# An LSTM beside an FFN on one core: four gates in one PSUM bank, cell operands in the other, weight sums on GpSimd

## The chip, the cores and the metric

The kernel runs on one core of a Trainium2 chip. A core has a matrix engine (TensorE, "PE" in the profile, with its weight loads as "PEld"), VectorE ("DVE"), ScalarE ("ACT"), GpSimd ("POOL") and a queue engine for transfers (SyncE, "SP"). They work side by side and wait for each other through semaphores. SBUF is the on-chip working memory; PSUM is a smaller one of eight banks of 512 fp32 columns on 128 partitions, into which TensorE writes its sums. The metric is the device time of one execution in microseconds; the kernel before takes 307.32 us (median of 3 runs, 306.71 to 307.52).

## What is computed

An LSTM of 64 steps over 32 sequences with 256 features, then a three-layer FFN whose weights are +1 or -1 on every output of the LSTM, and a residual. Cut to what matters:

```python
def step(carry, xw_t):                    # xw_t = x_t @ Wx + b
    prev_h, prev_c = carry
    a = xw_t + prev_h @ Wh                # 32 x 1024: gates i, f, o, g of 256 each
    i, f, o = sigmoid(a[:, :H]), sigmoid(a[:, H:2*H]), sigmoid(a[:, 2*H:3*H])
    g = tanh(a[:, 3*H:])
    next_c = f * prev_c + i * g
    next_h = o * tanh(next_c)
    return (next_h, next_c), next_h
...
h = concatenate([y, -y])                  # y: the LSTM's outputs
h = relu(s0 * (h @ W0)) * 2               # W: +1 / -1 from booleans
h = relu(s1 * (h @ W1)) * 2               # 1024 x 1024
return x + s2 * (h @ W2)
```

## The kernel before

**Layout.** The 256 features of a state are four quarters `q` of 64 columns. A quarter lies on 32 partitions (one for each sequence), so a cell tile is 128 partitions x 64 columns. The gate products of a step take the transposed state `hT` as 32-column weights and stream columns of `wh` past them; quarter `q` writes partitions 32q to 32q+31, so four such products run in TensorE beside each other. The gates stand in the order g, i, f, o (`GATES`, L60), each of 64 columns.

**Two gate banks.** `gate_banks` (L301) are two whole PSUM banks. The first holds g, i and f (192 columns used), the second o (64 columns). `gates_from_x` (L317) lets ScalarE copy the input's share of the step, `xg`, into both banks ahead of time (L319, L320), and `gates_from_h` (L304) adds `h @ Wh` onto it (L308): for each bank, each half `k` of the contraction and each quarter `q` one product, 16 a step. TensorE does an fp32 product in two passes, and the trace has a record for each. `cell_step` (L322) follows: the sigmoids of i and f (`sig`, L325), the tanh of g (`cand`, L326), the sigmoid of o (L327) on ScalarE; `kept` = f * c (L329), `new` = i * g (L331), their sum `c` (L333) on VectorE; `th` = tanh(c) on ScalarE (L335); `h` = o * th (L337) and its transpose into `hist` (L342) on VectorE. All tiles of the cell are in SBUF.

**What fills the time beside the recurrence.** The loop over t (L767) writes the engines' order by hand: each step issues its gate products and its cell, then as many pieces of other work as bring `done` up to a `goal` proportional to t. Up to step 20 (`X_STEPS` is 21) that is the products of x with Wx (`x_products`, L275; products of 128x256 at L249, evicted by `evict_x`, L261). From step 21 on it is the FFN (L777): four blocks of 16 time steps, with the layers at L425, L679 and L666. An FFN activation is kept as two fp32r parts, high and low, and each weight meets both. `split_h` (L347) makes the two parts of four steps of history: the high part on ScalarE (L361), the low part by a subtraction on VectorE (L362). The last two blocks (`last_blocks`, L442) do the second layer with fewer products: they use sums and differences of quarters of `w1`, which `make_sum` (L401) forms on VectorE, 16 instructions of 128x512 (L418).

**Small jobs.** `load` (L240) counts VectorE's extra work in a step. Splits and other small jobs go out where it is under 2; sums of w1 go out last in a step, from step 28 (`SUM_STEP`) on, while it is under 2 (L799 to L801). GpSimd does only the scalars and a few small loads at the start.

After step 63 nothing of the recurrence is left, and the rest of `last_blocks` runs to the end. There the two gate banks serve as product banks (`four_banks`, L446).

Of the kernel before, what the change touches and what calls it, by code (L numbers as in the profile page):

```python
# [34 lines left out]
F32 = mybir.dt.float32  # L35
F32R = mybir.dt.float32r
U8 = mybir.dt.uint8
AF = mybir.ActivationFunctionType
ALU = mybir.AluOpType
# [4 lines left out]
def lstm_ffn(ctx: ExitStack, tc: tile.TileContext, x, cond, wx_d, wh_d, b_d, k0_d, k1_d, k2_d, s0_d, s1_d, s2_d, out):  # L44
    nc = tc.nc
    P = 128
    N, T, D = x.shape
# [3 lines left out]
    HQ = H // NQ  # L51
# [6 lines left out]
    SH = 4  # L58
# [4 lines left out]
    X_STEPS = 21  # L63
# [5 lines left out]
    SUM_STEP = 28  # L69
# [7 lines left out]
    cell = ctx.enter_context(tc.tile_pool(name="cell", bufs=2))  # L77
# [6 lines left out]
    def act(shape, dtype, name):  # L84
        return apool.tile(shape, dtype, tag="act", name=name)
# [77 lines left out]
    for i in range(2):  # L163
        t = act([P, 2, F0], U8, f"k0_{i}")
# [75 lines left out]
    load = [0]  # L240
# [58 lines left out]
    hist, hparts = {}, {}  # L299

    gate_banks = [ps_g.tile([P, TB], F32, tag=f"gates{n}", name=f"gates{n}") for n in (3, 1)]  # L301
    gates = [g[:, : n * HQ].rearrange("p (g j) -> p g j", j=HQ) for g, n in zip(gate_banks, (3, 1))]

    def gates_from_h(t, hT):  # L304
        for g, slots in zip(gates, (slice(0, 3), slice(3, 4))):
            for k in range(2):
                for q in range(NQ):
                    nc.tensor.matmul(  # L308
                        g[q * N : (q + 1) * N],
                        hT[:, k, :],  # L310
                        wh_q[:, k, q, slots],
                        start=False,
                        stop=(k == 1),
                        skip_group_check=True,
                    )

    def gates_from_x(t):  # L317
        x_t = xg[t // 2 * 2][:, t % 2].rearrange("p (g j) -> p g j", g=4)
        nc.scalar.copy(gates[0], x_t[:, :3])  # L319
        nc.scalar.copy(gates[1], x_t[:, 3:])  # L320

    def cell_step(t, c):  # L322
        sig = cell.tile([P, 3, HQ], F32, tag="sig", name=f"sig{t}")
        cand = cell.tile([P, HQ], F32, tag="cand", name=f"cand{t}")
        nc.scalar.activation(sig[:, 0:2, :], gates[0][:, 1:3], AF.Sigmoid)  # L325
        nc.scalar.activation(cand, gates[0][:, 0], AF.Tanh)  # L326
        nc.scalar.activation(sig[:, 2, :], gates[1][:, 0], AF.Sigmoid)  # L327
        kept = cell.tile([P, HQ], F32, tag="kept", name=f"kept{t}")
        nc.vector.tensor_mul(kept, sig[:, 1, :], c)  # L329
        new = cell.tile([P, HQ], F32, tag="new", name=f"new{t}")  # L330
        nc.vector.tensor_mul(new, sig[:, 0, :], cand)  # L331
        c = cell.tile([P, HQ], F32, tag="c", name=f"c{t}")
        nc.vector.tensor_add(c, kept, new)  # L333
        th = cell.tile([P, HQ], F32, tag="th", name=f"th{t}")
        nc.scalar.activation(th, c, AF.Tanh)  # L335
        h = cell.tile([P, HQ], F32, tag="h", name=f"h{t}")
        nc.vector.tensor_mul(h, sig[:, 2, :], th)  # L337
        i, s = divmod(t, SH)
        if s == 0:
            hist[i] = hpool.tile([P, 2, SH * N], F32, tag="hist", name=f"hist{i}")  # L340
        hT = hist[i][:, :, ts(s, N)]
        nc.vector.transpose(hT, h.rearrange("p (j b) -> p b j", b=2))  # L342
        if t + 1 < T:
            gates_from_x(t + 1)
        return c, hT

    def split_h(i):  # L347

        b, s = divmod(i, SB // SH)
        if s == 0:  # L350
            hparts[b] = (
                hpool.tile([P, 2, TB], F32R, tag="hhi", name=f"hhi{b}"),
                hpool.tile([P, 2, TB], F32R, tag="hlo", name=f"hlo{b}"),
            )
        hi, lo = (p[:, :, ts(s, SH * N)] for p in hparts[b])
        full = hist.pop(i)
        if b == NB - 1:

            hi, lo = (a.rearrange("p k (n t) -> p k t n", n=N) for a in (hi, lo))
            full = full.rearrange("p k (t n) -> p k t n", n=N)  # L360
        nc.scalar.copy(hi, full)  # L361
        nc.vector.tensor_tensor(lo, full, hi, ALU.subtract)  # L362


    def evict(p, name):
# [35 lines left out]
    def make_sum(s, k):  # L401

        a11, a21 = w1[:, k, :F2], w1[:, k, F2:]
        a12, a22 = w1[:, K2 + k, :F2], w1[:, K2 + k, F2:]
        if s == 4:
            if k == 0:

                sums[s] = wpool.tile([P, K2, F2], F32R, tag="wx", name="s4")
            t = sums[s][:, k]
        else:  # L410
            t = act([P, F2], F32R, f"s{s}_{k}")
        in0, in1, op = {
            1: (a21, a22, ALU.add),
            2: (sums.get((1, k)), a11, ALU.subtract),
            3: (a11, a21, ALU.subtract),
            4: (a12, sums.get((2, k)), ALU.subtract),
        }[s]
        nc.vector.tensor_tensor(t, in0, in1, op)  # L418
        sums[s, k] = t

    f, parts = {}, {"b11": {}, "b21": {}}
# [294 lines left out]
    c = cell.tile([P, HQ], F32, tag="c", name="c_first")  # L716
# [28 lines left out]
    for _ in x_products(SB // 2, AHEAD):  # L745
        pass
    gates_from_x(0)


    def ffn():  # L750
        for b in range(NB - 2):
            yield from ffn_block(b)
        yield from last_blocks(NB - 2)
# [6 lines left out]
    sum_parts = deque(lambda s=s, k=k: make_sum(s, k) for k in range(K2) for s in range(1, 5))  # L760
# [6 lines left out]
    for t in range(T):  # L767
        load[0] = 0
        gates_from_h(t, hT)
        c, hT = cell_step(t, c)  # L770
        if t % SH == SH - 1:
            splits.append(t // SH)
        if outputs:
            load[0] += 1
            if next(outputs[0], "end") == "end":
                outputs.popleft()
        if t == X_STEPS:  # L777
            work, done = ffn(), 0
        goal = (t + 1) * total_x // X_STEPS if t < X_STEPS else (t + 1 - X_STEPS) * total_ffn // (T - X_STEPS)
        while done < goal:  # L780
            left_over[0] = goal - done
            done += next(work)
        if t == X_STEPS - 1:
            next(work, None)

        if turns and load[0] < 2:
            next_x(turns.popleft())
        if splits and (load[0] < 2 or t == T - 1 or t == SH * splits[0] + 2 * SH - 1):
            split_h(splits.popleft())
        else:  # L790
            if t >= FIRST_CHORE and chores:
                part = chores.popleft()()
                if part is not None:
                    w0_parts.append(part)
            elif t >= W2_STEP and chores2:
                chores2.popleft()()
            if w0_parts and (load[0] < 2 or t == X_STEPS - 1):
                w0_parts.popleft()()
            while sum_parts and t >= SUM_STEP and load[0] < 2:  # L799
                load[0] += 1  # L800
                sum_parts.popleft()()  # L801
    assert not sum_parts
    for _ in work:
        if outputs and next(outputs[0], "end") == "end":
# [29 lines left out]
```

## Time and profile before

| | |
|---|---|
| median of 3 runs | 307.32 us (306.71 to 307.52) |
| the profiled execution | 307.09 us, span 305.3 us from the first to the last instruction |
| granted TensorE clock | 1.000 |
| stretch to 16.7 us | start, loads, first products of x |
| 16.7 to 80.1 us | steps 0 to 20, beside the products of x |
| 80.1 to 231.4 us | steps 21 to 62, beside the FFN (step 63 begins at 231.4) |
| 231.4 to 300.6 us | the last blocks without the recurrence |
| VectorE busy in 80.1 to 231.4 | 88.1 of 151.3 us |
| ScalarE busy in 80.1 to 231.4 | 80.7 of 151.3 us |
| GpSimd busy after 12 us | nothing until the closing semaphores |

How to read the views: the page gives each engine's busy time, share of the span and number of instructions, and then the chain of work that ended last, by engine and line. The chain in order of time has start, length and what ran. A row of the groups has line, engine, operation, output<-inputs, shape and count, then busy us, mean ns of one, and the idle time before it. A row of the timeline has start, length, engine, line, operation, output<-input, shapes, and in brackets how long the engine had been idle before and what it waited for. Matmuls are pipelined: a row's length holds its latency too, and the distance between starts is what it costs.

### The profile page before, as it was taken

The numbers are of one execution on the slowest core, as the hardware profiler recorded it, in microseconds if no ns is written. First come the engines' busy times: TensorE is split into PE (matmuls) and PEld (weight loads), VectorE is DVE, ScalarE is ACT, GpSimd is POOL, SyncE is SP. The second block draws the span as 40 slices with busy tenths as digits, with TensorE's granted clock in tenths as the row PEclk, the third lists the DMA queues.
The fourth block names the chain that finished last, engine by engine and source line by source line (L and its number), as shares of the span: only waits on it lengthen the run. The fifth ranks groups of instructions, "written<-read, shape, count | busy, mean of one in ns | idle before, by whom it ended". The sixth has DMA issues, their size and how long they took to land.

```text
span 305.3 us, 9553 instructions
## 1 busy us (share of the span) xinstructions
PE 299.3 (98%) x4010; PEld 233.8 (77%) x4010; DVE 187.8 (62%) x527; ACT 154.9 (51%) x526; POOL 6.6 (2%) x24
## 2 busy tenths in 40 slices
PE   8999999999999999999999999999999999999993
PEld 4988887787777777777777777777777888888893
DVE  2476767676774565666575746444456689796341
ACT  0224657784565654444453544655676688644100
POOL 5300000000000000000000000000000000000000
PEclk9999999999999999999999999999999999999999
DMA  6865001133000000000001000000001330000012
GB/s 182 210 181 114 20 10 48 32 84 84 4 0 2 2 2 1 2 2 1 2 2 38 19 18 2 0 2 3 3 0 37 91 83 0 0 0 2 0 51 88
DMA packets 27450, 10.87 MB, mean 36 GB/s; under 512 B 23560, under 2 KB 26632, under 8 KB 27408
## 3 DMA queue, kind: packets, MB, share of 16 engines
q1 hardware_dynamic: 24768, 8.66, 11.5%
q10 hardware_dynamic: 2400, 1.57, 1.8%
q8 instruction: 31, 0.51, 0.7%
q0 software_dynamic: 240, 0.04, 0.1%
q14 instruction: 11, 0.09, 0.1%
HBM read 8.16 MB, written 2.10 MB: 34 GB/s over the span
## 4 chain that ended last, share of the span: by engine, by line
PE 98%; DVE 0%; issue 0%
PE p L679 21%; PE gates L308 20%; PE px L249 18%; PE q L452 12%; PE p L425 9%; PE po L666 5%; PE po L629 2%; PE gates L452 2%; PE po L617 2%; PE r L452 2%; PE gates L425 1%; PE p_idle L708 1%; PE gates L706 0%; DVE o L637 0%; PE p_bias L723 0%; DVE idle L113 0%
## 5 line engine op out<-in xcount | busy, mean ns | idle before, releaser
L308 PEld LDWEIGHTS gates<-wh,hist 128*32 128x32 f32 x2016 | 54.6, 109 | 22.3 <-issue 7.8
L308 PE MATMUL gates<-wh,hist 128*32 128x192 f32 x2016 | 68.1, 275 | 0.0
L249 PE MATMUL px<-wx,xT 128*32 128x256 f32 (+1 forms) x1168 | 60.5, 353 | 0.1
L249 PEld LDWEIGHTS px<-wx,xT 128*32 128x32 f32 x1168 | 42.4, 110 | 11.4 <-DVE c_first L717 0.8
L325 ACT ACTIVATE sig<-gates 128x128 f32<-128x128 f32 x64 | 17.7, 277 | 60.7 <-PE gates L308 60.4
L329 DVE TENSOR_TENSOR kept<-sig,c 128x64 f32<-128x64 f32 x63 | 14.2, 225 | 32.4 <-ACT sig L325 32.1
L335 ACT ACTIVATE th<-c 128x64 f32<-128x64 f32 x64 | 16.4, 257 | 32.2 <-DVE c L333 32.2
L337 DVE TENSOR_TENSOR h<-sig,th 128x64 f32<-128x64 f32 x64 | 14.4, 225 | 20.7 <-ACT th L335 20.7
L265 DVE TENSOR_TENSOR xg<-px,bias 128x512 f32<-128x512 f32 x32 | 21.2, 671 | 2.8 <-PE px L249 2.3
L425 PE MATMUL p<-hlo,w 128*128 128x512 f32 x56 | 22.5, 402 | 0.0
L425 PE MATMUL p<-hhi,w 128*128 128x512 f32 x56 | 22.3, 399 | 0.0
L319 ACT COPY gates<-xg 128x192 f32<-128x192 f32 x64 | 20.0, 313 | 0.6 <-DVE xg L265 0.6
L342 DVE STREAM_TRANSPOSE hist<-h 128x64 f32<-128x64 f32 x64 | 15.7, 246 | 2.6
L333 DVE TENSOR_TENSOR c<-kept,new 128x64 f32<-128x64 f32 x64 | 14.4, 225 | 2.2
L327 ACT ACTIVATE sig<-gates 128x64 f32<-128x64 f32 x64 | 14.9, 233 | 0.1
L331 DVE TENSOR_TENSOR new<-sig,cand 128x64 f32<-128x64 f32 x64 | 14.0, 218 | 0.0
L326 ACT ACTIVATE cand<-gates 128x64 f32<-128x64 f32 x64 | 14.0, 218 | 0.0
L320 ACT COPY gates<-xg 128x64 f32<-128x64 f32 x64 | 13.0, 203 | 0.0
L425 PEld LDWEIGHTS p<-hlo,w 128*128 128x128 f32 x56 | 10.5, 188 | 2.5
L425 PEld LDWEIGHTS p<-hhi,w 128*128 128x128 f32 x56 | 10.5, 188 | 2.4
L214 ACT ACTIVATE w<-bits,nsgn,sgn 128x1024 fp32r<-128x1024 uint8 x8 | 9.9, 1241 | 0.0
L362 DVE TENSOR_TENSOR hlo<-hist,hhi 128x256 fp32r<-128x256 f32 x16 | 7.5, 468 | 2.6 <-ACT hhi L361 2.6
(361 smaller groups left out, 573.4 us busy)
## 6 DMA issues: line engine op xcount, KB each, us to landing
x<-in_x_dram SPq DMA_DIRECT2D x52, 64.0 KB, 2.7
out_dram<-o SPq DMA_DIRECT2D x28, 64.0 KB, 1.8
bits<-in_L_ffn_k_dram SPq DMA_DIRECT2D x10, 128.0 KB, 3.4
wx<-in_L_cond_Wx_dram SPq DMA_DIRECT2D x2, 256.0 KB, 4.4
wx<-in_L_cond_Wx_dram ACTq DMA_DIRECT2D x4, 128.0 KB, 5.3
wh<-in_L_cond_Wh_dram ACTq DMA_DIRECT2D x2, 256.0 KB, 6.1
wh<-in_L_cond_Wh_dram SPq DMA_DIRECT2D x2, 256.0 KB, 6.8
k<-in_L_ffn_k_dram SPq DMA_DIRECT2D x2, 256.0 KB, 3.0
```

The source lines that it names most:

```text
L249: nc.tensor.matmul(p[q * N : (q + 1) * N, t % 2, slots], xT[i // 2, i % 2][:, s, k, :], wx_q[:, k, q, slots], start=start, stop=False, ski ...
L265: nc.vector.tensor_tensor(xg[t], p.rearrange("p t g j -> p t (g j)"), b, ALU.add)
L308: nc.tensor.matmul(g[q * N : (q + 1) * N], hT[:, k, :], wh_q[:, k, q, slots], start=False, stop=(k == 1), skip_group_check=True,)
L319: nc.scalar.copy(gates[0], x_t[:, :3])
L325: nc.scalar.activation(sig[:, 0:2, :], gates[0][:, 1:3], AF.Sigmoid)
L327: nc.scalar.activation(sig[:, 2, :], gates[1][:, 0], AF.Sigmoid)
L335: nc.scalar.activation(th, c, AF.Tanh)
L342: nc.vector.transpose(hT, h.rearrange("p (j b) -> p b j", b=2))
L425: nc.tensor.matmul(p, w0[:, k, ts(m, P)], a[:, k, :], start=(n == 0), stop=(n == 3))
L452: nc.tensor.matmul(bank, a(k)[:, ts(i, P)], b[k][n], start=first and k == 0 and n == 0, stop=k == K2 - 1 and n == 1, skip_group_check=True,)
L666: nc.tensor.matmul(po[m], w2[:, m, k], a1[k][n], start=(k == 0 and n == 0), stop=(k == FC1 - 1 and n == 1))
L679: nc.tensor.matmul(p1[m], w1[:, k, ts(m, P)], a0[k][n], start=(k == 0 and n == 0), stop=(k == FC0 - 1 and n == 1),)
```

## The change

From step 21 on, all four gates lie in the first bank (`rows`): `gates_from_h` issues 8 products of 256 columns instead of 8 of 192 and 8 of 64, and `gates_from_x` one copy instead of two. The second bank (`spare`) then serves as memory for the cell: the sigmoids of i and f, `kept` and `th` are written there instead of to SBUF. Up to step 20 both banks are used as before. In nine splits, those of steps 24 to 59, the low part is subtracted on GpSimd. All sums of w1 are formed on GpSimd, one a step from step 28 on, without regard to `load`.

```diff
-    gates = [g[:, : n * HQ].rearrange("p (g j) -> p g j", j=HQ) for g, n in zip(gate_banks, (3, 1))]
+    rows, spare = (g.rearrange("p (r j) -> p r j", j=HQ) for g in gate_banks)
+
+    def gate_parts(t):
+
+        if t < X_STEPS:
+            return (rows[:, :3], slice(0, 3)), (spare[:, :1], slice(3, 4))
+        return ((rows[:, :4], slice(0, 4)),)
 
     def gates_from_h(t, hT):
-        for g, slots in zip(gates, (slice(0, 3), slice(3, 4))):
+        for g, slots in gate_parts(t):
             for k in range(2):
                 for q in range(NQ):
                     nc.tensor.matmul(
...
     def gates_from_x(t):
         x_t = xg[t // 2 * 2][:, t % 2].rearrange("p (g j) -> p g j", g=4)
-        nc.scalar.copy(gates[0], x_t[:, :3])
-        nc.scalar.copy(gates[1], x_t[:, 3:])
+        for g, slots in gate_parts(t):
+            nc.scalar.copy(g, x_t[:, slots])
 
     def cell_step(t, c):
-        sig = cell.tile([P, 3, HQ], F32, tag="sig", name=f"sig{t}")
+        sig_o = cell.tile([P, HQ], F32, tag="sig", name=f"sig{t}")
         cand = cell.tile([P, HQ], F32, tag="cand", name=f"cand{t}")
-        nc.scalar.activation(sig[:, 0:2, :], gates[0][:, 1:3], AF.Sigmoid)
-        nc.scalar.activation(cand, gates[0][:, 0], AF.Tanh)
-        nc.scalar.activation(sig[:, 2, :], gates[1][:, 0], AF.Sigmoid)
-        kept = cell.tile([P, HQ], F32, tag="kept", name=f"kept{t}")
-        nc.vector.tensor_mul(kept, sig[:, 1, :], c)
         new = cell.tile([P, HQ], F32, tag="new", name=f"new{t}")
-        nc.vector.tensor_mul(new, sig[:, 0, :], cand)
+        h = cell.tile([P, HQ], F32, tag="h", name=f"h{t}")
+        if t < X_STEPS:
+            sig = cell.tile([P, 2, HQ], F32, tag="sig2", name=f"sig2_{t}")
+            kept = cell.tile([P, HQ], F32, tag="kept", name=f"kept{t}")
+            th = cell.tile([P, HQ], F32, tag="th", name=f"th{t}")
+            out_gate = spare[:, 0]
+        else:
+            sig, kept, th = spare[:, 2:4], spare[:, 4], spare[:, 5]
+            out_gate = rows[:, 3]
+        nc.scalar.activation(sig, rows[:, 1:3], AF.Sigmoid)
+        nc.scalar.activation(cand, rows[:, 0], AF.Tanh)
+        nc.scalar.activation(sig_o, out_gate, AF.Sigmoid)
+        nc.vector.tensor_mul(kept, sig[:, 1], c)
+        nc.vector.tensor_mul(new, sig[:, 0], cand)
         c = cell.tile([P, HQ], F32, tag="c", name=f"c{t}")
         nc.vector.tensor_add(c, kept, new)
-        th = cell.tile([P, HQ], F32, tag="th", name=f"th{t}")
         nc.scalar.activation(th, c, AF.Tanh)
-        h = cell.tile([P, HQ], F32, tag="h", name=f"h{t}")
-        nc.vector.tensor_mul(h, sig[:, 2, :], th)
+        nc.vector.tensor_mul(h, sig_o, th)
...
         nc.scalar.copy(hi, full)
-        nc.vector.tensor_tensor(lo, full, hi, ALU.subtract)
+        on = nc.gpsimd if X_STEPS < 4 * i < T - SH else nc.vector
+        on.tensor_tensor(lo, full, hi, ALU.subtract)
...
-        nc.vector.tensor_tensor(t, in0, in1, op)
+        nc.gpsimd.tensor_tensor(t, in0, in1, op)
         sums[s, k] = t
...
-            while sum_parts and t >= SUM_STEP and load[0] < 2:
-                load[0] += 1
-                sum_parts.popleft()()
+        if t >= SUM_STEP and sum_parts:
+            sum_parts.popleft()()
```

## The prediction

> **What bounds the kernel now.** I read four views: the page's busy shares, the chain that ended last, the groups of instructions by shape, and the timelines of one step. First the page, its busy times and its chain:
>
> ```profile
> span 305.3 us, 9553 instructions
> ...
> PE 299.3 (98%) x4010; PEld 233.8 (77%) x4010; DVE 187.8 (62%) x527; ACT 154.9 (51%) x526; POOL 6.6 (2%) x24
> ...
> PE 98%; DVE 0%; issue 0%
> ```
>
> TensorE (PE) is busy for 98% of the span and is 98% of the chain. Time is won only where a product gets shorter, and lost only where PE has to wait. The chain in order of time (start, length, what) shows the two kinds of step:
>
> ```profile
> 77.28 0.87 PE gates L308 x32
> 78.15 2.16 PE px L249 x40
> 80.31 0.87 PE gates L308 x32
> ...
> 98.16 1.01 PE gates L308 x32
> 99.17 2.49 PE p L679 x10
> 101.66 1.01 PE gates L308 x32
> 102.67 2.71 PE p L679 x11
> ```
>
> A step with FFN work is 1.01 us of gate products, then 10 or 11 FFN products of 0.227 us: 3.50 or 3.73 us, with no gap. There are 43 such steps (21 to 63). Each fp32 product is two records, so 16 products show as 32. The groups by shape (last columns: busy us, mean ns, idle before) name what the change replaces, and the form it uses instead:
>
> ```profile
> L308 PE MATMUL gates<-wh,hist 128*32 128x192 f32 x1008 | 54.1, 330 | 0.0
> L249 PE MATMUL px<-wx,xT 128*32 128x256 f32 x880 | 52.2, 379 | 0.0
> ...
> L308 PE MATMUL gates<-wh,hist 128*32 128x64 f32 x1008 | 26.2, 219 | 0.0
> ```
>
> Last the cell's own chain in one FFN step, ScalarE (ACT) and VectorE (DVE):
>
> ```profile
> 102.58 0.28 ACT L325 ACTIVATE sig<-gates 128x128 f32<-128x128 f32 x1
> ...
> 103.54 0.26 ACT L335 ACTIVATE th<-c 128x64 f32<-128x64 f32 x1 [0.45 <-DVE c L333]
> 103.70 0.31 ACT L319 COPY gates<-xg 128x192 f32<-128x192 f32 x1
> 103.95 0.20 ACT L320 COPY gates<-xg 128x64 f32<-128x64 f32 x1
> ```
> ```profile
> 104.09 0.24 DVE L342 STREAM_TRANSPOSE hist<-h 128x64 f32<-128x64 f32 x1
> ```
> ```profile
> 105.32 1.08 PE L308 MATMUL gates<-wh,hist 128*32 128x192 f32 x32
> ```
>
> The new state is ready at 104.33 and the gate products that read it start at 105.32: 0.98 us later. After a step of 10 products the same distance is 0.76. Where PE really waits for the transpose (the gate products at 49.79) it starts 0.15 after it. So the recurrence has 0.83 us to spare in steps of 11 products and 0.61 in steps of 10; some late steps have less (0.29 at 231.4, so 0.14 to spare), because a VectorE instruction stands in front of `kept`.
>
> **The change, part by part.**
>
> *Gate products, PE, on the path.* The records run four abreast (q = 0 to 3). In the step at 105.32 the groups of four start at 105.320, .506, .669, .831 (192 columns), .994, 106.050, .106, .161 (64 columns): 0.163 for 192 columns, 0.056 for 64, and 0.024 more for the first. Before: 4 x 0.163 + 4 x 0.056 = 0.873. After: four groups of 256 columns. The px products have that form, columns and operand layout: 2.16 us for 40 records is 0.216 a group, 4 x 0.216 = 0.864. The columns streamed stay the same; what goes is four group starts of 2.4 ns. That is 9.5 ns a step, and 43 x 9.5 ns = **0.41 us**. The cost of the change between full products and 32-column products (first gate record 0.319 after the last FFN product instead of 0.227; 0.149 from the last group's start to the FFN; 0.336 instead of 0.227 behind that) stays, as both kinds of product stay. Bounds: nothing saved, or 33.5 ns a step (the 0.024 of the first group gone too), 1.44 us.
>
> The Trainium skill, TensorEngine Tiling (Array Packing), section Instruction Overhead, says that each matmul carries about 60 cycles of overhead. By that, as an estimate, 16 records fewer would be 0.4 us a step and 17 us in all; the rows above contradict it, as 64-column groups of four records start every 56 ns, in proportion to their columns.
>
> *Later sigmoid, ACT, off the path.* Today `sig` starts when the three-gate bank is complete, while the fourth gate still streams: last record of that bank at 105.851, 326 ns long, `sig` at 106.30, 0.12 after its end. With one bank the last record starts at 105.32 + 0.24 + 2 x 0.216 + 0.02 = 106.01 and lasts 0.38 (the px row), so `sig` starts at 106.51: **0.21 us later** in each of 43 steps. Behind it in ACT's queue stand `cand`, the output gate, and later `th`, the gate copy and evictions. Cover: 0.61 to 0.83 us. Without cover it would be 43 x 0.21 = 9 us. In the late tight steps `kept` waits for a 0.69 us VectorE instruction and not for `sig` (at 229.71, 0.46 after the sigmoid's end), which absorbs the shift.
>
> *Operands in PSUM.* `th` from SBUF to SBUF takes 0.257; ACT copies of the same 64 columns into PSUM take 0.203: 0.05 gained on the cell's chain. The VectorE instructions `kept`, `new`, `c` and `h` now read one operand from PSUM, and `kept` writes it. No row shows a 64-column one. Nearest: 128x512 from PSUM (`xg`, L265) 671 ns against 681 from SBUF (L418), so about nothing; I take nothing. Upper end: no row reaches the double (0.45 instead of 0.225), 0.9 us on the chain; lower end: the same 10 ns a piece saved, unseen behind PE.
>
> *One gate copy instead of two, ACT, off the path:* 0.31 and 0.20 overlapping, about 0.45 together, become one of 256 columns, about 0.37 by the step between those rows. PE waits for the transpose later than for the copy in every step, so nothing.
>
> *Sums of w1 (16 instructions of 0.65 to 0.68 on VectorE) and 9 of the splits' low parts (0.42, three of them 0.62) go to GpSimd (POOL).* VectorE loses 16 x 0.67 + 6 x 0.42 + 3 x 0.62 = 15 us of its 187.8, none of it on the chain: worth nothing by itself. POOL is idle after 12 us. On POOL the nearest row is a 128x1 TENSOR_TENSOR of 0.19, on VectorE 0.67: between 0.19 and some multiple of 0.67 each. The sums are first read behind step 63; w1 was written by 69 us. The low parts wait for `hhi` and are read by layer 0: the tightest is the one at 119.26, read from 123.27 on, 3.6 us after its end. POOL is strictly in order, so up to four sums follow each low part; none stands in front of that one for long. The history buffer is written again four steps after a low part. The last split, which PE reads 0.3 us after it, stays on VectorE. The rate of sums, now one a step and no longer counted in `load`, comes last in its step and moves no other instruction.
>
> The Trainium skill, SBUF — State Buffer, section Who interferes with whom, speaks against this part: a VectorE instruction with two SBUF inputs and a GpSimd instruction that reads SBUF exclude each other for their whole length; with one PSUM operand they don't. By it the four cell products escape from step 21 on, and the first GpSimd instruction comes later than that. No row here shows it, as POOL is idle.
>
> **Sum.** 307.09 (the profiled execution; span 305.3 and 1.79 around it) - 0.41 = 306.68. Its time is 0.23 below the median of the runs, 307.32; against that median: **306.9 us**.
>
> **Rivals.**
> 1. *Faster: the first group's 24 ns go as well, or the entry into the gates gets shorter with half the weight loads.* For: 8 loads are issued in front of the second group. Against: the first load of each of the four columns stays. Price 1.44 us: 305.9.
> 2. *Slower: POOL holds up the cell on VectorE.* For: the cell's four VectorE instructions lie on the recurrence, and 25 POOL instructions fall into steps 27 to 60. Against: each of them has a PSUM operand now. Price: if each POOL instruction holds the cell once for its VectorE length, the chain grows by 0.21 - 0.05 + 0.68 = 0.84 in 16 steps, over the cover by 0.23 in steps of 10 products and 0.01 in steps of 11, together 1.9 us, and some 0.1 for the three long low parts: 307.3 - 0.4 + 2.0 = 308.9. It decides from holds of 0.45 us (0.61 - 0.16). At twice the VectorE length it would be over 320.
> 3. *Slower: PSUM operands on VectorE are dear.* It decides from 0.11 us each (4 x 0.11 + 0.16 = 0.61). At 0.15 each the 10-product steps, some 23, are late by 0.15: 3.5 us, 310.4. Against: 671 against 681 ns.
> 4. *The change does nothing on PE:* half the records, same streaming and no start cost saved: 307.3.
>
> **How the numbers follow.** Forecast 0.55 (its own range 306.5 to 307.3), rival 4 0.10, rival 1 0.15, rival 2 0.12, rival 3 0.08. A measurement of this kernel can tell about 0.3%, 0.9 us, from no change. Forecast and rival 4 lie within it: same 0.65. Rival 1 is faster: 0.15. Rivals 2 and 3: slower 0.20. The range goes from rival 1's price with a little noise, 305.8, to that of rival 2, 308.8; the dearer ends of 2 and 3 are left out.
>
> **What would show it.** Right: the gate pieces of the FFN steps at 1.00 instead of 1.01 with 16 records, four groups 0.216 apart; `sig` 0.21 later against the first gate record; no wait of PE for `hist`; POOL rows between 105 and 222 us; the distance from transpose to gates still over 0.3 in the usual steps. Wrong: gate records that start 0.15 behind a transpose (2 or 3; the VectorE cell rows say which, stretched while POOL runs or stretched always), or a gates piece well under 0.98 (1).

## The result and the profile after

The changed kernel takes 308.69 us (median of 6 runs, 308.27 to 309.10) against 307.29 us for the one before (6 runs). The ratio is 1.0048, with an interval of 1.0035 to 1.0061: **slower by 1.40 us**, where 0.4 us less was forecast. The profiled execution took 308.97 us. Of the executions told below, one of e10_twelve (763.53 us, the profiled one) and one of e12_six (1048.21 us) were slow; the medians of these two kernels count them, the ratios don't. The page's busy times and its chain:

```profile
span 307.2 us, 8208 instructions
...
PE 300.7 (98%) x3322; PEld 217.6 (71%) x3322; DVE 178.6 (58%) x502; ACT 151.0 (49%) x483; POOL 33.7 (11%) x49
...
PE 98%; DVE 0%; issue 0%
```

PE has 688 records fewer (43 steps of 16), and yet it is busy 1.4 us longer. VectorE has lost 9 us, GpSimd has gained 27. The chain is still PE, so the time was lost inside PE's own sequence. The chain in order of time (start, length, what) shows where:

```profile
98.54 1.00 PE gates L314 x16
99.54 2.53 PE p L692 x10
102.07 1.00 PE gates L314 x16
103.07 2.73 PE p L692 x11
```

The gate products are 1.00 instead of 1.01, as forecast. But the ten FFN products behind them, which the change doesn't touch, take 2.53 instead of 2.49, and the eleven 2.73 instead of 2.71. The steps of x are as before (gates 0.87, products 2.16). One step in the timeline (start, length, engine, line, operation; in brackets the idle time before):

```profile
103.00 0.50 PE L692 MATMUL p<-a_7h,w 128*128 128x512 f32 x1
...
103.19 0.26 ACT L341 ACTIVATE gates<-gates 128x128 f32<-128x128 f32 x1 [0.34 <-ACT w L218]
...
103.33 0.39 PE L692 MATMUL p<-a_7l,w 128*128 128x512 f32 x1
...
103.48 0.23 DVE L344 TENSOR_TENSOR gates<-gates,c 128x64 f32<-128x64 f32 x1 [0.51 <-ACT gates L341]
...
103.82 0.23 DVE L345 TENSOR_TENSOR new<-gates,cand 128x64 f32<-128x64 f32 x1
...
104.39 0.23 ACT L348 ACTIVATE gates<-c 128x64 f32<-128x64 f32 x1 [0.70 <-DVE c L347]
...
104.56 0.36 ACT L326 COPY gates<-xg 128x256 f32<-128x256 f32 x1
...
104.91 0.24 DVE L354 STREAM_TRANSPOSE hist<-h 128x64 f32<-128x64 f32 x1
...
105.73 0.42 PE L314 MATMUL gates<-wh,hist 128*32 128x256 f32 x4
```

The sigmoids, `kept` and `th` now carry the bank's name, `gates`. The state is ready at 105.15 (104.91 + 0.24) and is read at 105.73: 0.58 us later instead of 0.98. In steps of 10 products it is 0.37 instead of 0.76. PE starts `a_7l` 0.33 behind `a_7h`, as before, but the distances after that don't fall to 0.227 at once.

**Where the time went.** I cut each profiled execution into stretches: from the span's start to the first gate record of step 22, from there to that of step 63 (41 steps), from there to the start of the last matmul (tail), and from there to the end. All in us:

| | to step 22 | 41 steps | tail | end | span |
|---|---|---|---|---|---|
| before | 83.63 | 147.81 | 68.84 | 4.99 | 305.27 |
| after | 83.94 | 148.83 | 68.91 | 5.51 | 307.19 |
| difference | +0.30 | +1.02 | +0.07 | +0.52 | +1.92 |

The first stretch varies from 83.34 to 84.33 over the profiled executions of this study, in no order with the edits (it holds the first loads), so its 0.30 isn't taken as an effect. The other three sum to 1.61. The ratio's interval, times 307.3, is 1.08 to 1.87 us, so they account for it. The 0.52 stands apart: it is read from the profiled executions, and is smaller than the width of that interval.

### The profile page after: what moved, and what is told of

Its sections match the earlier page's. It is cut to its first block, busy times and chain, and to the rows that moved or that the text cites. A ratio compares the mean times of both kernels' runs of the same rounds, so it can differ in the third digit from the quotient of the medians.

```text
span 307.2 us, 8208 instructions
## 1 busy us (share of the span) xinstructions
PE 300.7 (98%) x3322; PEld 217.6 (71%) x3322; DVE 178.6 (58%) x502; ACT 151.0 (49%) x483; POOL 33.7 (11%) x49
## 4 chain that ended last, share of the span: by engine, by line
PE 98%; DVE 0%; issue 0%
PE p L692 21%; PE gates L314 20%; PE px L249 18%; PE q L465 12%; PE p L438 9%; PE po L679 5%; PE po L642 2%; PE po L630 2%; PE r L465 2%; PE gates L465 2%; PE gates L438 1%; PE p_idle L721 1%; PE gates L719 0%; DVE o L650 0%; PE p_bias L736 0%; DVE idle L113 0%
## 5 line engine op out<-in xcount | busy, mean ns | idle before, releaser
L314 PE MATMUL gates<-wh,hist 128*32 128x256 f32 (+2 forms) x1328 | 67.7, 331 | 0.0
L314 PEld LDWEIGHTS gates<-wh,hist 128*32 128x32 f32 x1328 | 38.9, 109 | 24.4 <-issue 4.7
L341 ACT ACTIVATE gates<-gates 128x128 f32<-128x128 f32 x43 | 11.3, 262 | 41.9 <-PE gates L314 33.7
L344 DVE TENSOR_TENSOR gates<-gates,c 128x64 f32<-128x64 f32 x43 | 10.0, 232 | 34.9 <-ACT gates L341 34.7
L326 ACT COPY gates<-xg 128x256 f32<-128x256 f32 (+1 forms) x85 | 24.9, 309 | 1.7 <-DVE xg L265 1.7
L348 ACT ACTIVATE gates<-c 128x64 f32<-128x64 f32 x43 | 9.8, 228 | 31.3 <-DVE c L347 31.3
L341 ACT ACTIVATE sig<-gates 128x128 f32<-128x128 f32 x21 | 5.8, 277 | 19.5 <-PE gates L314 19.4
L343 ACT ACTIVATE sig<-gates 128x64 f32<-128x64 f32 x64 | 14.8, 232 | 0.1
L345 DVE TENSOR_TENSOR new<-gates,cand 128x64 f32<-128x64 f32 x43 | 9.7, 225 | 4.5
L347 DVE TENSOR_TENSOR c<-gates,new 128x64 f32<-128x64 f32 x43 | 9.7, 225 | 1.6 <-DVE new L345 0.2
L431 POOL TENSOR_TENSOR s<-w 128x512 fp32r<-128x512 f32 x8 | 10.3, 1288 | 0.0
```

Of the source, the lines that this page charges most:

```text
L314: nc.tensor.matmul(g[q * N : (q + 1) * N], hT[:, k, :], wh_q[:, k, q, slots], start=False, stop=(k == 1), skip_group_check=True,)
L326: nc.scalar.copy(g, x_t[:, slots])
L341: nc.scalar.activation(sig, rows[:, 1:3], AF.Sigmoid)
L343: nc.scalar.activation(sig_o, out_gate, AF.Sigmoid)
```

## The experiments

Each table row below gives the median with its number of runs, the ratio to the kernel before on the same chip with its interval, and the 41 steps and the end of its profiled execution (before: 147.81 and 4.99).

### Which part costs what

My theory after the first reading: the one-bank form disturbs PE's rhythm (the spacing of the FFN products behind the gates), and the cell's longer chain adds some waits. The rivals: GpSimd holds something up, or the PSUM operands do. Four kernels take the parts singly.

**e1_form**: the kernel before, with the one-bank form alone; the cell stays in SBUF and the sums on VectorE.

```diff
+    def gate_parts(t):
+        if t < X_STEPS:
+            return (gates[0], slice(0, 3)), (gates[1], slice(3, 4))
+        return ((row4, slice(0, 4)),)
...
-        for g, slots in zip(gates, (slice(0, 3), slice(3, 4))):
+        for g, slots in gate_parts(t):
```

> The kernel before with the gate form alone changed: from step 21 on one bank and 8 products of 256 columns; the cell stays in SBUF, sums and splits stay on VectorE. Theory (rhythm): the FFN products that follow the gates are paced by weight load and product, and take some products to settle at 227 ns; the four groups of 256 columns make them enter that settling at a worse place. Then the FFN steps take 3.53 us (10 products) and 3.735 us (11), and the time is 308.0 to 308.3. Rival (PSUM operands slow the products, or GpSimd does): neither is here, so the steps take 3.49 and 3.72 and the time is 306.9.

**e2_two_banks**: the kernel after, without the one-bank form: 16 products into two banks in every step. The cell's operands then share the second bank with the output gate.

```diff
     def gate_parts(t):
-        if t < X_STEPS:
-            return (rows[:, :3], slice(0, 3)), (spare[:, :1], slice(3, 4))
-        return ((rows[:, :4], slice(0, 4)),)
+        return (rows[:, :3], slice(0, 3)), (spare[:, :1], slice(3, 4))
...
-            out_gate = rows[:, 3]
+            out_gate = spare[:, 0]
```

> The changed kernel with the gates back in two banks by products of 192 and 64 columns; cell operands stay in the second bank's other columns, sums and low parts stay on GpSimd. Theory (rhythm): FFN steps back at 3.50 and 3.73 us, apart from some late steps where the gates wait for the transpose; 307.3 to 307.6. Rival (PSUM operands or GpSimd slow the products): steps stay at 3.53 and 3.735, 308.6.

**e3_split**: the kernel after, all four gates in one bank, but by 16 products as before (192 columns, then 64).

```diff
+    def product_parts(t):
+        if t < X_STEPS:
+            return gate_parts(t)
+        return (rows[:, :3], slice(0, 3)), (rows[:, 3:4], slice(3, 4))
...
-        for g, slots in gate_parts(t):
+        for g, slots in product_parts(t):
```

> The changed kernel, all four gates in one bank, but by products of 192 and 64 columns as before. Theory (rhythm, set by the form of the products): 3.50 and 3.73 us, 307.3 to 307.6. If it is the bank and not the form: 3.53 and 3.735, 308.6. Rival (PSUM operands or GpSimd): 308.6 too.

**e4_pool**: the kernel before, with the sums (one a step, as in after) and the nine low parts on GpSimd and nothing else; the cell stays in SBUF.

```diff
-        nc.vector.tensor_tensor(lo, full, hi, ALU.subtract)
+        on = nc.gpsimd if X_STEPS < 4 * i < T - SH else nc.vector
+        on.tensor_tensor(lo, full, hi, ALU.subtract)
...
-        nc.vector.tensor_tensor(t, in0, in1, op)
+        nc.gpsimd.tensor_tensor(t, in0, in1, op)
...
```

> The kernel before with the GpSimd part alone: sums of w1 and nine low parts on GpSimd, cell in SBUF, gates as before. Theory (a VectorE instruction with two SBUF operands and a GpSimd instruction exclude each other): the cell's instructions wait for sums of 1.28 us in five bursts of 4 to 6 GpSimd instructions, the gates wait for the transpose in some 7 to 10 steps by 0.5 to 3 us each: 310 to 322. Rival (they don't exclude each other): 307.3, cell rows unchanged. If GpSimd alone slows the FFN products: 308 or more with cell rows unchanged.

| | median, us | ratio | 41 steps | end |
|---|---|---|---|---|
| e1_form | 307.82 (5) | 1.0022 (1.0010 to 1.0035) | 148.63 | 4.98 |
| e2_two_banks | 309.12 (5) | 1.0066 (1.0054 to 1.0078) | 149.19 | 5.50 |
| e3_split | 308.28 (6) | 1.0043 (1.0025 to 1.0062) | 148.25 | 5.51 |
| e4_pool | 318.25 (6) | 1.0366 (1.0335 to 1.0397) | 157.68 | 5.36 |

**e1** has eight products less in each step, nothing of the cell in PSUM and no work moved to GpSimd, and it alone loses 0.81 of the 1.02 us in the 41 steps. Its chain has the pieces of after:

```profile
99.01 2.53 PE p L687 x10
101.54 1.00 PE gates L315 x16
102.54 2.73 PE p L687 x11
```

So neither the PSUM operands nor GpSimd is needed for this part. **e3** keeps all that after has except the shape of the products. Its steps without a wait are 3.50 and 3.73 again:

```profile
98.89 2.49 PE p L697 x10
101.38 1.01 PE gates L319 x32
102.39 2.71 PE p L697 x11
```

The products, then, are the cause, and not the bank. Of the 0.44 us that e3 still loses, 0.32 is gates that wait for the state (first record 0.41, 0.41, 0.37 and 0.41 instead of 0.32 behind the last FFN product at 187.9, 202.4, 209.8 and 231.6); most of the rest is in the distances behind. The times of e3 and e2 missed the 307.3 to 307.6 that I had expected of both.

**e2** tells that a bank that holds both a gate and the cell's operands is dear: `kept` starts 1.75 us behind the first gate record instead of 1.48. It reads no output gate, but it starts 0.03 us behind the end of the output gate's sigmoid, which reads the bank that `kept` writes; the view by source line names that sigmoid (L341) in 27 of the steps and an FFN product in three. In most steps of 10 products the gates then start 0.15 behind the transpose. Its 41 steps are the longest of these but for e4, although the rhythm of its products is that of before.

**e4** is rival 2 of the prediction at its full price. VectorE and GpSimd in the steps where both work:

```profile
107.07 0.50 DVE L329 TENSOR_TENSOR kept<-sig,c 128x64 f32<-128x64 f32 x1 [1.21 <-ACT sig L325]
...
107.74 1.20 DVE L333 TENSOR_TENSOR c<-kept,new 128x64 f32<-128x64 f32 x1
109.26 0.91 DVE L337 TENSOR_TENSOR h<-sig,th 128x64 f32<-128x64 f32 x1 [0.32 <-ACT th L335]
```
```profile
106.21 1.27 POOL L419 TENSOR_TENSOR s<-w 128x512 fp32r<-128x512 f32 x1
107.57 1.29 POOL L419 TENSOR_TENSOR s<-s,w 128x512 fp32r<-128x512 f32 x1
108.82 1.27 POOL L419 TENSOR_TENSOR s<-w 128x512 fp32r<-128x512 f32 x1
```

A 64-column instruction that takes 0.22 otherwise takes 0.50, 1.20 and 0.91: `kept` ends with the first sum (107.5), `c` with the second (108.9), `h` near the end of the third (110.1). PE waited four times for the transpose, 7.9 us in all, at most 2.8.

### The longer chain of the cell

How far behind the first gate record each instruction of the cell starts, in the steps near 100 us (us):

```
        sig   kept  new   c     th    h     transpose
before  0.98  1.30  1.44  1.69  1.95  2.24  2.50
e1      1.20  1.51  1.65  1.90  2.16  2.45  2.71
after   1.19  1.48  1.82  2.08  2.40  2.66  2.91
e7      1.19  1.48  1.62  1.87  2.19  2.45  2.70
```

e1 shows the forecast's 0.21 and nothing more. In after `new` starts 0.34 behind `kept` instead of 0.14: it waits until `kept` has written, though it doesn't read `kept`. What they share is the bank: `new` reads the sigmoid from the bank that `kept` writes. The wait stands in the program. At the line of `new`, after has a semaphore instruction of VectorE in each of the 43 steps, which before and e7 (below) don't have there:

```profile
L345 DVEq EVENT_SEMAPHORE  x43: 21/21/21, 82.2 to 234.5; - x43
```

No run shows what the bank would do without it. (`th` too has one such instruction more, on ScalarE, in after and e7, and starts 0.06 later behind `c`.)

**e7_kept**: the kernel after with `kept` in SBUF.

```diff
-            sig, kept, th = spare[:, 2:4], spare[:, 4], spare[:, 5]
+            sig, th = spare[:, 2:4], spare[:, 5]
+            kept = cell.tile([P, HQ], F32, tag="kept", name=f"kept{t}")
```

> The changed kernel with the product of forget gate and cell state in SBUF, the sigmoids and the tanh still in the second bank. Theory (a read of a bank waits for the write into the same bank before it): the product of input gate and candidate no longer waits for it, the cell's chain is 0.19 us shorter, the distance from transpose to gates grows from 0.38 and 0.58 us to 0.56 and 0.76, and the four late waits of the gates (at 189, 203.6, 210.9, 232.8 us) go: 0.2 us, 308.5. The sum of the two products now has both operands in SBUF and may wait for GpSimd once in a few steps, within the cover. Rival (the wait has another cause): distances unchanged.

Measured: 309.38 us (6 runs), ratio 1.0068 (1.0051 to 1.0086); 41 steps 149.47, end 5.49. The 0.20 is gone (last row of the table), and the state is ready 0.56 and 0.78 us ahead of the gates, nearly as in e1 (0.57 and 0.78). Also gone are the four waits by which after exceeds e1: its gates enter 0.394, 0.380, 0.342 and 0.381 us behind the last FFN product at 189.0, 203.6, 210.9 and 232.8, against 0.323 as e1's mean; together 0.21 us. They came about in steps where the cell was late for another reason, 0.27 us in the first of them (`sig` at 1.46 instead of 1.19 behind the gates), so that 0.20 more was over the cover; in the second and the fourth `kept` starts at 1.77, behind another VectorE instruction, as it does in before. And yet the 41 steps of e7 are longer than those of after (149.47 against 148.83), and its time is above the 308.5 that I had expected, since `c` now adds two SBUF operands:

```profile
121.67 1.14 DVE L348 TENSOR_TENSOR c<-kept,new 128x64 f32<-128x64 f32 x1
```
```profile
121.45 1.29 POOL L432 TENSOR_TENSOR s<-w 128x512 fp32r<-128x512 f32 x1
```

`c` ends with the sum on GpSimd, near 122.8, and the gates of that step enter 0.915 behind the last FFN product (123.9), 0.612 in another (156.8). One SBUF operand too many on one instruction of the chain is enough for the hold of e4; I had taken it to stay within the cover. Putting `kept` into PSUM is thus a bargain with two sides: 0.20 us on the chain in every step against two holds.

### What sets the products' rhythm

The mean of each part of a step over the 41 steps (ns): from the first gate record to the first FFN product; from the last FFN product to the first gate record (entry); from the first FFN product to the second; what the later distances exceed 226.67 by, together; and the sum. e1 and e3 are told above, the others below.

| | gates to FFN | entry | second | later excess | sum |
|---|---|---|---|---|---|
| before | 1010.9 | 318.6 | 336.7 | 20.9 | 1687.1 |
| e5_o_first | 1010.7 | 318.5 | 336.7 | 21.1 | 1687.0 |
| e6_halves | 1010.9 | 318.3 | 336.7 | 20.7 | 1686.6 |
| e14_eight_by_k | 1010.9 | 318.5 | 336.6 | 21.0 | 1687.1 |
| e3_split | 1010.9 | 324.7 | 336.9 | 23.0 | 1695.5 |
| e1_form | 1000.9 | 322.7 | 337.8 | 45.0 | 1706.4 |
| e9_61_columns | 1000.8 | 322.6 | 337.9 | 45.1 | 1706.4 |
| after | 1001.0 | 326.2 | 337.8 | 45.2 | 1710.1 |
| e12_six | 1005.9 | 322.6 | 335.7 | 29.5 | 1693.7 |
| e13_ten | 1015.9 | 327.0 | 340.8 | 52.6 | 1736.4 |
| e10b_twelve | 1020.7 | 322.7 | 337.9 | 45.2 | 1726.4 |

(The entries of e3 and after hold their waits for the state.) In before the distances behind the gates are 337, 236, 228, 233, 231, 226, 227, 227, 226 ns. In after and e1 they are 341, 240, 235, 233, 236, 224, 231, 236, 228 in one step and 335, 229, 233, 236, 224, 231, 236, 228, 233, 231 in the next. From 233, 236, 224 on the second list is the first one moved by a place; where it reads 236, 228, 233, 231 at its end, that is how before's list begins, and there 226 and 227 follow. In the tail, where no gates interrupt it, after's sequence ends so too (232, 231, 227, 227, 226). All three are thus one fixed sequence, entered at different places: before enters it late and is settled after five distances, after and e1 enter it earlier and are interrupted before it settles.

Seven kernels ask what decides the place: the number of records, the order of the pieces, the bank, or only the stage's length.

**e5_o_first**: before, with the output gate's products ahead of the other three gates in the FFN steps.

```diff
-        for g, slots in zip(gates, (slice(0, 3), slice(3, 4))):
+        parts = list(zip(gates, (slice(0, 3), slice(3, 4))))
+        for g, slots in parts if t < X_STEPS else parts[::-1]:
```

> The kernel before with the order of its two banks turned round in the steps with FFN work: the o gate's products of 64 columns first, those of 192 columns last. The columns, the weight loads and the number of products stay. Theory (rhythm): what counts is the moment, to some nanoseconds, at which the gates let the FFN products start again. The gates stage is as long as before (1.01 us), so the products should enter the settling where they did: 3.50 and 3.73 us, 307.0. If it is the width of the last group (192 or 256 against 64): 3.53 and 3.735, 307.8.

**e6_halves**: e1, with two products of 128 columns in place of each of 256.

```diff
...
+        return (row4[:, :2], slice(0, 2)), (row4[:, 2:], slice(2, 4))
...
```

> All four gates in one bank, the cell in SBUF and everything else as before, but by 16 products of 128 columns, so eight groups of four. By the groups' starts the gates stage is as long as with 192 and 64 (8 starts). Theory (rhythm set by the stage's length): 3.50 and 3.73 us, 307.0. If the width of the last group sets it: 3.53 and 3.735, 307.8. If one bank for all gates is what costs: 307.8 as well, and the last run would tell it from the width.

**e14_eight_by_k**: before, with both banks' products for the first half of the contraction ahead of those for the second (192, 64, 192, 64).

```diff
+        whole = list(zip(gates, (slice(0, 3), slice(3, 4))))
...
+        if t >= X_STEPS:
+            pieces = [(*p, k) for k in range(2) for p in whole]
+        for g, slots, k in pieces:
```

> The kernel before with its eight groups in another order: both banks for the first half of the contraction, then both for the second, so widths 192, 64, 192, 64. Columns, records and length as before. Theory (length decides): 3.50 and 3.73 us, 147.8 for the 41 steps, 307.3. Rival (the order or the last group's neighbours decide): anything else, 148.6 as with 256.

**e9_61_columns**: before with its 32 records, but the output gate's products 61 columns wide instead of 64, so that the stage is as short as e1's.

```diff
+        cut = 61 if slots.start == 3 and t >= X_STEPS else HQ
```

> The kernel before, but in the steps with FFN work the o gate's products take 61 of their 64 columns; the product of h with the last 3 columns of each quarter is left out. 32 records and weight loads as before, the stage some 10 ns shorter (4 groups x 3 columns x 2 passes at 2.4 GHz), so as long as with four groups of 256. Theory (the length of the gates stage, to some nanoseconds, decides where the FFN products enter their settling): steps of 3.53 and 3.735 us, 41 steps in 148.6 instead of 147.8, time 307.8. Rival (the number of records or weight loads in the stage decides): 3.49 and 3.72, 147.4, time 306.6.

**e12_six**: e1, with the second half of the contraction cut in two, so that a step has 12 products (256; 192, 64) and the stage lies between those of e1 and before.

```diff
+        pieces = [(g, slots, k) for g, slots in gate_parts(t) for k in range(2)]
+        if t >= X_STEPS:
+            pieces[1:] = [(row4[:, :3], slice(0, 3), 1), (row4[:, 3:], slice(3, 4), 1)]
...
```

> All four gates in one bank, cell in SBUF, rest as before; the first half of the contraction by 256 columns, the second by 192 and 64: six groups, 24 records, the stage half way (4.8 ns) between the kernel before and four groups of 256. Theory (length decides): entry and steps either as before (3.50, 3.73: 147.6 for the 41 steps) or as with four groups (3.53, 3.735: 148.6), nothing smooth between. Rival (each record or load saved costs a share): half way, 148.2.

**e10_twelve, e10b_twelve, e13_ten**: longer stages. e10 and e10b are one kernel, before with three pieces for each half of the contraction (128, 64, 64); e13 has two (192, 64) for the first and three for the second; the diff is that of e13. Where the steps are read, the trace is that of e10b.

```diff
+        whole = list(zip(gates, (slice(0, 3), slice(3, 4))))
+        fine = [(gates[0][:, :2], slice(0, 2)), (gates[0][:, 2:], slice(2, 3)), whole[1]]
...
+            pieces = [(*p, k) for k in range(2) for p in (whole, fine)[k]]
```

> The kernel before with 24 products a step instead of 16: g and i by 128 columns, f by 64, o by 64; 48 records, twelve groups of four, the stage by four group starts (9.5 ns) longer. Theory (length decides): the entry into the settling moves once more; where to can't be told beforehand. Without a move: 3.51 and 3.735, 307.4. With an entry nearer to the settled 227 ns it can fall under 147.8 for the 41 steps, by 0.8 us at most; with one as far as that of the four groups, 308.6. Rival (more records cost nothing but their start): 147.8 + 41 x 0.0095 = 148.2.

> The kernel before with twelve groups of four in the gates stage (g and i by 128 columns, f by 64, o by 64), 9.5 ns longer; taken again, since the profile of the first try fell into a disturbed execution. Its median was 308.9 against 307.4. Theory (length decides the entry into the settling): the steps show it, 3.53 us or more for 10 products and a settling that enters early, 149.0 to 149.4 for the 41 steps. Rival (more records cost only their starts): settling as in the kernel before, 148.2.

> The kernel before with ten groups of four: the first half of the contraction by 192 and 64 columns, the second by 128, 64 and 64; the stage 4.8 ns longer. Theory (length decides): between eight and twelve groups; the entry either stays (148.0 for the 41 steps), or alternates from step to step as with six groups (148.1 to 148.6). If it enters nearer to the settled pace it falls to 147.2 to 147.7, and the time beats both kernels: 306.5 to 306.9.

| | median, us | ratio | 41 steps | end |
|---|---|---|---|---|
| e5_o_first | 307.02 (12) | 0.9989 (0.9978 to 1.0000) | 147.82 | 4.99 |
| e6_halves | 307.28 (12) | 0.9995 (0.9983 to 1.0007) | 147.81 | 4.98 |
| e14_eight_by_k | 307.15 (11) | 0.9993 (0.9984 to 1.0002) | 147.82 | 4.98 |
| e9_61_columns | 307.92 (11) | 1.0023 (1.0005 to 1.0042) | 148.63 | 4.99 |
| e12_six | 307.40 (12) | 1.0001 (0.9983 to 1.0018) | 148.11 | 4.97 |
| e13_ten | 309.21 (7) | 1.0049 (1.0031 to 1.0067) | 149.85 | 4.98 |
| e10_twelve | 308.86 (7) | 1.0045 (1.0029 to 1.0060) | | |
| e10b_twelve | 309.15 (6) | 1.0055 (1.0037 to 1.0073) | 149.44 | 4.97 |

The three kernels with a stage of 1010.9 ns agree with before to 0.5 ns a step, in other orders, other widths and in one bank. e9 is the strongest: it has twice e1's records and weight loads, two banks and fewer columns, only the length is the same, and its steps equal e1's to 0.1 ns. Its chain beside that of e1 above:

```profile
98.56 1.00 PE gates L309 x32
99.56 2.53 PE p L680 x10
102.09 1.00 PE gates L309 x32
103.09 2.73 PE p L680 x11
```

It computes less than before and takes longer. **The stage's length decides, to some nanoseconds**, and not the records, the loads or the columns. That is shown for 1010.9 and 1000.9, which several forms share; the other three lengths have one form each. Nor is "longer is better" true: 1015.9 gives the worst of all, 149.85 for the 41 steps where I had expected 148.6 at most, and 1020.7 the same distances as 1000.9. e12 (1005.9) alternates between the two entries, and its 41 steps are 0.3 us above before, within its interval. That nothing lies between the two times, as I had expected, missed: a stage in between gave a time in between, if by alternation. Nothing here beats the kernel before by more than its interval.

What stays open is which quantity sets the place in the sequence. The lengths 20 ns apart (1000.9 and 1020.7) agree and those 5 or 10 ns apart don't, which would fit a period, but these runs are too few to fix one. Nor was it tried with another kind of product behind the stage.

### The end of the program

Behind the last matmul after takes 5.51 us instead of 4.99. In the closing instructions GpSimd stands idle between the clearing of its semaphores and its last drain. The groups of those two in after (durations min/median/max in ns, first and last start):

```profile
L842 POOLq DRAIN  x3: 102/183/1559, 223.0 to 306.8; - x3
...
L842 POOLq EVENT_SEMAPHORE_RANGE_CLEAR  x1: 139/139/139, 306.2 to 306.2; - x1
```

And in before:

```profile
L830 POOLq DRAIN  x3: 40/102/911, 11.5 to 305.0; - x3
...
L830 POOLq EVENT_SEMAPHORE_RANGE_CLEAR  x1: 139/139/139, 304.8 to 304.8; - x1
```

By the unrounded starts they are 0.525 us apart, against 0.168 in before, and the last drain takes 0.183 instead of 0.040: 0.36 and 0.14 of the 0.52. Two kernels ask whether one instruction of GpSimd late in the program brings this, or their number.

**e8_one_pool**: before, with a single low part (that of steps 56 to 59) on GpSimd.

```diff
-        nc.vector.tensor_tensor(lo, full, hi, ALU.subtract)
+        on = nc.gpsimd if i == 14 else nc.vector
+        on.tensor_tensor(lo, full, hi, ALU.subtract)
```

> The kernel before with one single low part, that of steps 56 to 59, on GpSimd. Theory (the end of the program takes longer on GpSimd once it has done an instruction of this kind): the time from GpSimd's clearing of the semaphores to its next closing instruction is 0.52 us instead of 0.17, and the time 0.4 to 0.5 us longer with FFN steps unchanged: 307.4. Rival (the longer end comes from many GpSimd instructions, or by chance): end unchanged, 307.0.

**e11_fewer_low**: after, with three of the nine low parts back on VectorE.

```diff
-        on = nc.gpsimd if X_STEPS < 4 * i < T - SH else nc.vector
+        on = nc.gpsimd if X_STEPS < 4 * i < T - 4 * SH else nc.vector
```

> The changed kernel with the last three of GpSimd's nine low parts (steps 48 to 59) back on VectorE: some five records fewer in GpSimd's stream. Theory (GpSimd stands still for some 0.4 us behind the 68th record of its stream, and in the changed kernel this falls into the closing sequence): the clearing of the semaphores is now before the 68th record, the time from it to the next closing instruction is 0.17 instead of 0.52, and the end 4.98 instead of 5.51: 308.2, FFN steps as in the changed kernel but for one to three late waits. Rival (the longer end comes from the number of GpSimd instructions of this kind): end stays at 5.5.

e8: 307.14 us (12 runs), ratio 0.9993 (0.9983 to 1.0002), 41 steps 147.81, end 4.99. My expectation that one instruction lengthens the end **fell**. e11: 308.55 us (8 runs), 1.0042 (1.0027 to 1.0057), 41 steps 148.83 as in after, end 4.98:

```profile
L842 POOLq DRAIN  x3: 46/93/1427, 178.7 to 306.7; - x3
...
L842 POOLq EVENT_SEMAPHORE_RANGE_CLEAR  x1: 142/142/142, 306.5 to 306.5; - x1
```

0.171 us apart. The shorter end shows in the profile only: by the runs e11 is 0.14 us below after, which the intervals don't tell from nothing, and above the 308.2 that I had expected. Counted over all records of GpSimd's stream, after, e2, e3 and e7 have 71 and stand still behind the 68th, the clearing; e4 has 70 and stands still, 0.36 us, behind the 68th too, which there is the drain; e11 (67), e8 (41), before and e1 (39) don't stand still. So the count in the stream goes with the stop in these nine kernels, and a single instruction on GpSimd doesn't bring it. That the instructions have to be fetched there is my explanation; it was only argued.

## Why the prediction was wrong

**The step that failed** is the sentence "The cost of the change between full products and 32-column products [...] stays, as both kinds of product stay". The saving of 9.5 ns a step in the stage itself came nearly to the nanosecond (1010.9 to 1001.0, so 9.9). But the prices around the stage were taken from one stage of one length and treated as constants: with the shorter stage the entry, the second distance and the later distances cost 4.1 + 1.1 + 24.1 ns more (e1 against before), so a step gains 10 and loses 29: +19 ns, 0.8 us in the 41 steps. The forecast was a gain of 0.41 in all 43. The profile of before couldn't say that, but it had a hint that I passed over: the distances behind the gates weren't 227 but 236, 228, 233, 231 before they settled. (The 0.149 in that sentence of the prediction is measured from the last record's start; from the last group's it is 0.170. Nothing rests on it.)

**The cell's chain** was sized at 0.21 - 0.05 = 0.16 and is 0.41 longer (transpose at 2.91 instead of 2.50). The sigmoid's 0.21 was right, and alone would have cost no wait (e1). The step "so about nothing; I take nothing" for PSUM operands was right for the durations (`kept` 0.232, `new` and `c` 0.225, `h` 0.221 us on average) and wrong about the waits that come with a shared bank: `new` waits for `kept`, 0.20. `th` gave back nothing of its 0.05 where it counts: it is shorter by 0.03, but starts 0.06 later behind `c`. Cover was left in the usual steps, as said (0.37 and 0.58); the late steps, whose shift I took to be absorbed, had none for the 0.20: 0.21 us. (The sigmoid's shift was absorbed in the steps at 200.0 and 229.2, where `kept` starts at 1.77 as in before.)

**The end** had no term in the sum. It is 0.52 in the profiled execution, and goes with the number of GpSimd's instructions (e8 and e11, which have fewer, don't show it).

**Rival 2** named the right mechanism for the wrong kernel: with SBUF operands it costs 9.9 us in the 41 steps (e4), with one instruction exposed two waits (e7), and with one PSUM operand in each cell instruction nothing: in after no cell row is stretched while a sum of 1.29 us runs. **Rival 3** (PSUM operands dear by duration) fell with the rows above. **Rival 1** fell: the first group's 24 ns stayed and the entry became longer. The upper end of the range, 308.8, was to be the price of rival 2, which had been worked out as 308.9; nothing rests on that either. Sums on GpSimd take 1.29 us instead of 0.67 and come in time. VectorE's busy time fell by 9.2 us, not by the 15 forecast, and bought nothing, as said. Its rows' lengths add up to 14.8 us less (203.8 to 189.0), as forecast; but busy time counts rows that overlap once, and fewer of them overlap now, `new` and `kept` for one (0.08 us in each of 43 steps).

Two rules of the Trainium skill were weighed. TensorEngine Tiling (Array Packing), section Instruction Overhead, has about 60 cycles a matmul. Taken as a cost on top of every matmul, as the prediction took it, the runs go against it: 16 records fewer gave 10 ns a step (e1), and 32 records with the same length gave the same time (e9). Its own example, that one column takes as long as 60, makes it a floor for narrow products; the narrowest here have 61 columns, so no run tests that. SBUF — State Buffer, section Who interferes with whom, has the exclusive lock between a VectorE instruction with two SBUF inputs and GpSimd: e4 and e7 agree (0.22 us became 0.50 to 1.20), and after agrees from the other side.

## What to carry to other kernels

A stage that interrupts a stream of matmuls can have a price that depends on its length to some nanoseconds, in the products behind it: try a few lengths of the same work on the chip before believing a saving of 1% of the stage, and read the distances behind it and not only the stage. An operand moved to PSUM escaped GpSimd here, but instructions that touch the same bank then waited for each other: give what is written and what is read at the same time different banks, or count the wait. And before work goes to an idle GpSimd, look which VectorE instructions on the recurrence read two operands from SBUF.

## What the runs showed of the hardware

- 128x512 products behind 32-column ones need up to ten places to settle at 226.7 ns, and lose 21 to 53 ns on the way behind the first two, by the stage's length (1010.9 against 1000.9, 1015.9, 1020.7 ns).
- GpSimd stands still for some 0.36 us more than usual behind the 68th record of its stream in the five kernels that have more than 68 (four times the clearing, once a drain).
- In e4 PE stood idle for 2.4 us until 127.6. Behind that the gates took 1.36 us to the last record's start instead of 0.86, three FFN products followed at 0.43 us each, and the granted clock of the stretch 124 to 132 us is 0.79; the stretches of 8 us before and behind it have 1.00. So this wait cost more than its own length. The longest one of that run, 2.8 us until 146.5, did not: the gates behind it took 0.86 and the clock stayed at 1.00. What tells the two apart may be where the wait falls. PE was busy for 1.02 of the 3.40 us from 124.5 to 127.9, and the granted clock was 0.50 for the 3.40 us behind that; of the longer wait two such stretches, from 141.56 and from 144.97, each have a part, with PE busy for 2.12 and 1.93 us. One such event is too few to show it.
